# A two-layer graph network on one core: four edits to the last thirty-five microseconds

## The chip, the core and the metric

The kernel runs on one core of one Trainium2 chip. A core has TensorE (matrix products), VectorE (DVE in the profile), ScalarE (ACT), GpSimd (POOL) and SyncE (SP), each with its own queue of instructions, and DMA engines that move data between DRAM and on-chip memory. SP and ACT issue plain DMAs; POOL issues indirect ones, which gather or scatter rows by an index. The metric is the device time of one execution in microseconds (us).

## The reference

32 graphs (batches), each with 512 nodes of 512 features, share one adjacency matrix. What matters of the reference is this:

```python
def _layernorm(x): ...           # mean 0, variance 1 along the features, eps 1e-5
# layer 0
h = max(layernorm(x), 0)
x = x + (adj @ h) @ weight + bias
# layer 1: attention, 8 heads of 64 features
h = max(layernorm(x), 0)
q, k, v = h @ Wq + bq, h @ Wk + bk, h @ Wv + bv          # split into heads
scores = q k^T / 8 + (1 - adj) * -1e9
x = x + (softmax(scores) @ v) @ Wo + bo
return x                          # float32 (32, 512, 512)
```

The entries of `adj` lie between 0 and 1, and in each row of this data the largest stands well clear of the second, so the term with 1e9 leaves, in each row of scores, one node that counts. Layer 1 is then a lookup: node n takes `h[idx[n]] @ (Wv @ Wo)` plus a constant row, where `idx[n]` is the node with the largest entry in row n.

## The kernel before

The kernel first looks at `adj` and computes whether the lookup is exact for it. If so it takes `single_path`, otherwise `general_path`, a full attention. Here it takes `single_path`, and the profile is of that.

`single_path` handles one batch after another, software-pipelined. Layer 0 is two 512x512x512 products per batch. Each is done by `product`: seven products of half-size blocks with sums and differences of blocks, named p1, p5, u2, c11, c22, c12, c21. p1 opens PSUM bank u, p5 bank v and c11 a third; u2, c22 and c21 accumulate onto u, c12 onto v. After each piece, a `take` function moves the bank to its place: p1, p5, u2 and c21 with ScalarE, c11, c22 and c12 with an addition on VectorE (`take_z`, for layer 1).

Layer 1 uses the fact that only at most 352 (32 x 11) different nodes are looked up. `put_h` scatters the rows of h to DRAM so that those come first, `get_h` fetches them, `transpose_h` turns them, `layer1` computes z^T = (Wv Wo)^T h^T plus the constant into `ZT` with `product`, 176 columns at a time, `put_z` transposes z^T on VectorE into `ZR` and stores it to DRAM in four DMAs per call (one for each group of 32 partitions), for columns of blocks s0 to s1: 0 to 6 and 6 to 11. `finish` gathers the rows of z from DRAM by `place` and adds them to x. Near the end `fetch` gathers without adding, into free tiles (`late_z`: batch 29 into `sel`, batch 30 into `yT`), and `add_z` adds on VectorE and stores the batch's output.

The last batch, 31, does without that detour: `put_h` stores h unsorted, `get_all` gathers all 512 rows by `idx` into `hs[0]`, `transpose_all(r)` transposes 128 rows of it on TensorE, with a copy by ScalarE into `hs[1]`, and `layer1_rows` makes the four 128x512 row blocks of the last product, with an addition into x on VectorE and a store on SP for each.

The order of everything is written by hand, and each engine runs its instructions in the order in which they are written down. Per batch b, a list `todo` has 21 steps, seven for layer 0, seven for the next aggregation, seven for layer 1 of the batch before; `put(batch, step, f)` hangs work on a step. `run` writes down the matrix products of piece k, then the work of step k, then the `take` of piece k. In the last two rounds, b = 31 and b = 32, that gives this order:

- steps 7 to 13 of b = 31: layer 1 of batch 29. Step 13 holds `put_z(29, 6, 11)`, `get_all(31)` and two block sums; then c21 is taken by ScalarE.
- steps 14 to 20 of b = 31: layer 1 of batch 30. Step 14 (p1) holds `put_z(29, 0, 6)`, step 15 `fetch(29)`, steps 15 to 18 an addition of a constant row to x of batch 31 (`add_cvo`), step 20 (c21) `put_z(30, 6, 11)`. Step 18 belongs to c22.
- b = 32: `transpose_all(0)`, `put_z(30, 0, 6)`, `fetch(30)`, and at last `layer1_rows(31)`.

`work` is a pool with one buffer for each name: two tiles of the same name share their memory, and the second is not written before the last read of the first. `ZT` of every batch has the name "zs", and `H0S`, block sums of layer 0, "h0s". POOL's queue holds, in this order, `get_all` (four gathers), `fetch(29)` (four) and `fetch(30)` (four).

Of the kernel before, what the change touches and what calls it, by code (L numbers as in the profile page):

```python
# [8 lines left out]
F32 = mybir.dt.float32  # L9
# [8 lines left out]
P = 128  # L18
# [3 lines left out]
S = 11  # L22
# [3 lines left out]
def gnn_two_layers(ctx: ExitStack, tc: tile.TileContext, x, adj, w0, b0, wq, bq, wk, bk, wv, bv, wo, bo, out):  # L26
# [150 lines left out]
    with tc.If(single > P - 1) as cmp:  # L177
        single_path(tc, x, wv, bv, wo, bo, out, kept)
# [38 lines left out]
def single_path(ctx: ExitStack, tc: tile.TileContext, x, wv, bv, wo, bo, out, kept):  # L217
# [15 lines left out]
    nc = tc.nc  # L233
    B, N, D = x.shape
    C, DC = N // P, D // P
# [6 lines left out]
    work = ctx.enter_context(tc.tile_pool(name="work", bufs=1))  # L242
# [6 lines left out]
    PUT, H0S, H1, HS, HC, HT, HTS, Z, ZT, ZR = {}, {}, {}, {}, {}, {}, {}, {}, {}, {}  # L249
# [10 lines left out]
    def sum_a(s, t, i):  # L260
        a11, a12, a21, a22 = blk(t, 0, 0), blk(t, 1, 0), blk(t, 0, 1), blk(t, 1, 1)
        if i == 0:
            nc.vector.tensor_add(s[:, 0], a21, a22)
        elif i == 1:
            nc.vector.tensor_sub(s[:, 1], s[:, 0], a11)
        elif i == 2:
            nc.vector.tensor_sub(s[:, 2], a11, a21)
        else:
            nc.vector.tensor_sub(s[:, 3], a12, s[:, 1])
# [12 lines left out]
    def product(a, sa, bt, sb, take, half=HALF, pieces=("p1", "p5", "u2", "c11", "c22", "c12", "c21")):  # L282


        def gemm(bank, lhs, rhs, first):
            for m in range(2):
                for k in range(2):
                    nc.tensor.matmul(bank[:, m, 0:half], lhs[:, k, m * P:(m + 1) * P], rhs[:, k, :],  # L288
                                     start=(first and m == 0 and k == 0), stop=(k == 1), skip_group_check=True)

        u, v, w = None, None, None
        for piece in pieces:
            if piece == "p1":
                u = bank = ps_m.tile([P, 2, HALF], F32, name="mm")
                gemm(u, blk(a, 0, 0), blk(bt, 0, 0, half), True)
            elif piece == "p5":
                v = bank = ps_m.tile([P, 2, HALF], F32, name="mm")
                gemm(v, sa[:, 0], sb[:, 0], True)
            elif piece == "u2":
                bank = u  # L300
                gemm(u, sa[:, 1], sb[:, 1], False)
            elif piece == "c11":
                w = bank = ps_m.tile([P, 2, HALF], F32, name="mm")
                gemm(w, blk(a, 1, 0), blk(bt, 1, 0, half), True)
            elif piece == "c22":
                bank = u
                gemm(u, sa[:, 2], sb[:, 2], False)
            elif piece == "c12":
                bank = v
                gemm(v, sa[:, 3], blk(bt, 1, 1, half), False)  # L310
            else:
                bank = u
                gemm(u, blk(a, 1, 1), sb[:, 3], False)
            meanwhile = yield
            for f in meanwhile or ():
                f()
            take(piece, bank[:, :, 0:half])
# [12 lines left out]
    def take_z(t):  # L330
        def take(piece, bank):
            i, k = PLACE[piece]
            dst = blk(t, i, k, WIDE)
            if piece in ("c11", "c22", "c12"):
                nc.vector.tensor_add(dst, bank, dst)
            else:
                for m in range(2):
                    nc.scalar.activation(dst[:, m, :], bank[:, m, :], AF.Identity,  # L338
                                         bias=cvo_c[:, 2 * i + m:2 * i + m + 1])
        return take  # L340
# [75 lines left out]
    def places():  # L416
        table = dram.tile([N, 1], I32, name="table", bufs=1)
        nc.sync.dma_start(table.rearrange("(c p) o -> p (c o)", p=P), dest)
        return table

    def look_up(table):
        for c in range(C):
            nc.gpsimd.indirect_dma_start(
                out=place[:, c:c + 1], out_offset=None, in_=table,
                in_offset=bass.IndirectOffsetOnAxis(ap=idx[:, c, 0:1], axis=0))
# [67 lines left out]
    def transpose_all(r):  # L493
        pt = ps_t.tile([P, DC, P], F32, name="pt")
        for d in range(DC):
            nc.tensor.transpose(pt[:, d, :], hs[0][:, r, d * P:(d + 1) * P], ident)
        nc.scalar.copy(hs[1][:, :, r * P:(r + 1) * P], pt)
# [4 lines left out]
    def layer1_rows(b):  # L502
        for r in range(C):
            bank = ps_m.tile([P, D], F32, name="mm")
            for d in range(DC):
                if d == 2 and r + 1 < C:
                    transpose_all(r + 1)
                nc.tensor.matmul(bank, hs[1][:, d, r * P:(r + 1) * P], wvo[:, d, :], start=(d == 0), stop=(d == DC - 1))  # L508
            for bz, c in ((), ((B - 3, 0), (B - 3, 1)), ((B - 3, 2), (B - 3, 3)), [(B - 2, c) for c in range(C)])[r]:
                add_z(bz, c, nc.sync if bz == B - 3 else nc.scalar)  # L510
            x_r = X[b][:, r, :].rearrange("p (q c e) -> p q c e", q=4, c=4)
            nc.vector.tensor_add(x_r, bank.rearrange("p (c q e) -> p q c e", q=4, c=4), x_r)
            nc.sync.dma_start(out[b, r * P:(r + 1) * P, :], X[b][:, r, :])

    def transpose_h(b, r):
        if r == 0:
            HT[b] = adjT[:, :, 0:32 * S] if b == B - 2 else work.tile([P, DC, 32 * S], F32, name="hT")
        s0, s1 = 4 * r, min(4 * r + 4, S)
        nc.vector.transpose(HT[b][:, :, 32 * s0:32 * s1].rearrange("p c (s j) -> p s c j", j=32),
                            HC[b][:, s0:s1, :].rearrange("p s (c e) -> p s c e", c=4))  # L520
# [4 lines left out]
        sum_b(HTS[b], HT[b], i, WIDE)  # L525

    def layer1(b):
        ZT[b] = work.tile([P, DC, 32 * S], F32, name="zs")
        return product(wvo, wvo_t, HT[b], HTS[b], take_z(ZT[b]), WIDE)

    def put_z(b, s0, s1):
        if b not in Z:
            Z[b] = dram.tile([32 * S, D], F32, name="z")
            ZR[b] = work.tile([P, S, P], F32, name="hc" if b == B - 2 else "zr")
        nc.vector.transpose(ZR[b][:, s0:s1, :].rearrange("p s (c e) -> p s c e", c=4),  # L535
                            ZT[b][:, :, 32 * s0:32 * s1].rearrange("p c (s j) -> p s c j", j=32))
        rows = Z[b].rearrange("(s j) (q f) -> q j s f", j=32, q=4)
        for q in range(4):
            eng = nc.scalar if b == B - 2 and s0 == 0 and q > 1 else nc.sync
            eng.dma_start(rows[q][:, s0:s1, :], ZR[b][32 * q:32 * q + 32, s0:s1, :])  # L540

    def finish(b):
# [14 lines left out]
    def add_z(b, c, eng):  # L557
        nc.vector.tensor_add(X[b][:, c, :], late_z[b][:, c, :], X[b][:, c, :])
        eng.dma_start(out[b, c * P:(c + 1) * P, :], X[b][:, c, :])
# [23 lines left out]
    with tc.manual_schedule():  # L583
# [6 lines left out]
        for b in range(B + 1):  # L590
            todo = [[] for _ in range(21)]

            def put(batch, step, f, *args):
                if 0 <= batch < B:
                    todo[step].append(lambda: f(batch, *args))
# [9 lines left out]
            if b == B - 1:  # L605
                put(b - 2, 13, put_z, 6, S)
# [44 lines left out]
            put(b + 2, 17 + late, lambda b: ahead[0].offset())  # L651
            for c in range(C):
                put(b + 2, min(17 + late + c, 20), lambda b, c: ahead[0].relu(c), c)
            if b == 1:
                tables = []
                put(1, 0, lambda b: tables.append(places()))
                put(1, 11, lambda b: look_up(tables[0]))
                for step, i in ((4, 0), (4, 1), (5, 2), (5, 3)):
                    put(1, step, lambda b, i: sum_a(wvo_t, wvo, i), i)
            if b == 0:  # L660
                for step, c in ((0, 0), (0, 1), (1, 2), (2, 3)):
                    put(0, step, add_b0, c)
                for step, i in ((0, 0), (0, 1), (1, 2), (1, 3)):
                    put(0, step, lambda b, i: sum_b(adjT_s, adjT, i), i)
                todo[3] += todo[4] + todo[5] + todo[6]
                put(0, 11, lambda b: number_rows())
                for step, i in ((11, 0), (12, 1), (12, 2), (13, 3)):
                    put(0, step, lambda b, i: sum_b(w0_t, w0_s, i), i)
                for j in range(DC):
                    put(0, 16 + j, lambda b, j: bias_part(j), j)  # L670
                run(layer0_rows(0), todo[0:4])
            elif b < B:
                run(layer0(b), todo[0:7])
            else:
                transpose_all(0)
                run(None, todo[0:7])
            run(aggregate(b + 1) if b + 1 < B else layer1(b - 2) if b < B else None, todo[7:14])
            if b == 0:
# [268 lines left out]
```

## Time and profile before

| | |
|---|---|
| median of 3 runs | 1108.0 us (1107.43 to 1109.12) |
| the profiled execution | 1104.05 us |
| its span, first to last instruction | 1101.6 us |
| TensorE busy | 1079.9 us (98%) |
| VectorE busy | 907.3 us (82%) |
| ScalarE, GpSimd busy | 358.6 us (33%), 443.8 us (40%) |
| bytes moved by DMA | 186.90 MB, mean 170 GB/s |
| L288, matrix products of `product`, share of the chain that ended last | 89% |

The profile is one execution, recorded by the chip's profiler. PE is TensorE's matrix products, PEld its loading of weights; a number with L is a line of the kernel. In a row of the timeline, "[0.80 <-ACT zs L338]" says that the engine stood idle for 0.80 us and that ScalarE's line 338 ended this. A wait for several semaphores is put down to the one that came last. A DMA has two times: that of its issue on a queue (SPq, ACTq, POOL), and its landing, when all its bytes are there. The span is shorter than the execution by what lies before the first and after the last instruction, here 2.45 us.

### The profile page before, as it was taken

The page shows a single profiled execution, that of the slowest core. Times are in us where ns is not written, and L with a number is a line of the kernel's source. Part 1 is how long each engine was busy: PE and PEld are TensorE (multiplying, and loading weights), DVE is VectorE, ACT ScalarE, POOL GpSimd, SP SyncE. Part 2 cuts the span into 40 slices and gives each one's busy share as a digit, 9 for nine tenths or more (in the row PEclk, how much of TensorE's full clock was granted, in tenths as well). Part 3 has the DMA queues.
Part 4 walks back from the last instruction along what each step waited for, and adds up shares of the span by engine and source line. Part 5 has one row for each costly group of instructions (what it writes and reads, how often), then busy time and mean ns, then how long its engine had stood idle before and what let it go on. Part 6 is the DMA issues. An engine that isn't in the chain of part 4 may idle for free.

```text
span 1101.6 us, 15852 instructions
## 1 busy us (share of the span) xinstructions
PE 1079.9 (98%) x5404; PEld 953.2 (87%) x5404; DVE 907.3 (82%) x1853; ACT 358.6 (33%) x655; POOL 443.8 (40%) x491
## 2 busy tenths in 40 slices
PE   7999999999999999999999999999999999999996
PEld 3569989999989989988999998999999899999883
DVE  6869888888888888878888888888888878888863
ACT  3223323233323333322323332323332232333221
POOL 2124544333554343454333454433355434345413
PEclk9999999999999999999999999999999999999999
DMA  6362676667777667767666776666776766676537
GB/s 238 125 141 74 172 191 148 160 175 197 182 181 158 149 171 193 187 171 169 157 156 189 193 189 177 146 160 173 196 179 181 164 149 171 184 193 155 141 105 245
DMA packets 162412, 186.90 MB, mean 170 GB/s; under 512 B 14993, under 2 KB 102289, under 8 KB 162321
## 3 DMA queue, kind: packets, MB, share of 16 engines
q1 hardware_dynamic: 130672, 112.70, 37.3%
q0 software_dynamic: 27968, 66.61, 27.0%
q10 hardware_dynamic: 3680, 6.49, 1.7%
q8 instruction: 44, 0.72, 0.3%
q14 instruction: 48, 0.39, 0.2%
HBM read 96.28 MB, written 89.46 MB: 169 GB/s over the span
## 4 chain that ended last, share of the span: by engine, by line
PE 94%; DMA 1%; DVE 1%; ACT 1%; POOL 1%; issue 1%; ACTq 0%; SPq 0%; POOLq 0%; DVEq 0%
PE mm L288 89%; PE mm L139 1%; PE mm L458 1%; PE mm L372 1%; PE mm L508 1%; POOL x L544 1%; DMA x<-in_x_dram 1%; DMA yT<-z,place 1%; ACT h L212 0%; DMA z<-zr 0%; DVE x L345 0%; DVE st L194 0%; ACT zs L338 0%; POOL yT L553 0%; DVE zr L535 0%
## 5 line engine op out<-in xcount | busy, mean ns | idle before, releaser
L544 POOL DMA_INDIRECT x<-z,place x116 | 182.8, 1576 | 370.6 <-DMA z<-zr 318.7
L327 ACT COPY yT<-mm 128x512 f32<-128x512 f32 x124 | 71.8, 579 | 562.0 <-PE mm L288 527.9
L345 DVE TENSOR_TENSOR x<-mm,x 128x512 f32<-128x512 f32 x217 | 149.7, 690 | 86.2 <-PE mm L288 86.2
L212 ACT ACTIVATE h<-x,off,rstd 128x512 f32<-128x512 f32 x256 | 194.9, 808 | 36.2 <-DVE off L204 34.2
L201 POOL TENSOR_TENSOR rstd<-ve,mhalf 128x2 f32<-128x2 f32 (+1 forms) x97 | 106.0, 1093 | 222.1 <-DVE ve L200 222.1
L194 DVE BATCH_NORM_STATS2 st<-x 128x6 f32<-128x512 f32 x256 | 171.5, 670 | 9.2 <-DMA x<-in_x_dram 8.0
L288 PE MATMUL mm<-w_t,sel 128*128 128x256 f32 x744 | 171.1, 380 | 0.8 <-DVE x L345 0.8
L288 PE MATMUL mm<-adjT_s,h0s 128*128 128x256 f32 x744 | 170.8, 380 | 1.0 <-ACT yT L327 1.0
L288 PEld LDWEIGHTS mm<-w_t,sel 128*128 128x128 f32 x744 | 141.5, 191 | 20.4 <-DVE x L345 1.6
L288 PEld LDWEIGHTS mm<-adjT_s,h0s 128*128 128x128 f32 x744 | 141.6, 191 | 20.2 <-ACT yT L327 1.4
L470 POOL DMA_INDIRECT hs<-h,dest x124 | 133.7, 1078 | 30.8 <-issue 22.2
L338 ACT ACTIVATE zs<-mm,cvo_c 128x176 f32<-128x176 f32 x248 | 87.2, 403 | 98.2 <-PE mm L288 98.2
L288 PE MATMUL mm<-hTs,wvo_t 128*128 128x176 f32 x720 | 117.5, 313 | 0.6 <-ACT zs L338 0.6
L288 PE MATMUL mm<-adjT,h 128*128 128x256 f32 x496 | 117.2, 380 | 0.0
L288 PE MATMUL mm<-w_s,yT 128*128 128x256 f32 x496 | 117.2, 380 | 0.0
L288 PEld LDWEIGHTS mm<-hTs,wvo_t 128*128 128x128 f32 x720 | 109.8, 191 | 1.1 <-ACT zs L338 1.1
L288 PEld LDWEIGHTS mm<-adjT,h 128*128 128x128 f32 x496 | 94.5, 191 | 13.0 <-issue 0.5
L288 PEld LDWEIGHTS mm<-w_s,yT 128*128 128x128 f32 x496 | 93.3, 191 | 11.5 <-issue 0.5
L436 DVE TENSOR_TENSOR x<-x,b_r 128x512 f32<-128x512 f32 x128 | 86.6, 678 | 0.0
L288 PE MATMUL mm<-hT,wvo 128*128 128x176 f32 x480 | 81.4, 313 | 0.0
L288 PEld LDWEIGHTS mm<-hT,wvo 128*128 128x128 f32 x480 | 75.3, 190 | 1.5
L325 DVE TENSOR_TENSOR yT<-mm,yT 128x512 f32<-128x512 f32 x93 | 63.9, 687 | 5.8 <-PE mm L288 3.0
(146 smaller groups left out, 1278.9 us busy)
## 6 DMA issues: line engine op xcount, KB each, us to landing
out_dram<-x SPq DMA_DIRECT2D x124, 256.0 KB, 4.1
x<-in_x_dram SPq DMA_DIRECT2D x120, 256.0 KB, 5.5
hc<-hs SPq DMA_DIRECT2D x124, 176.0 KB, 3.8
z<-zr SPq DMA_DIRECT2D x120, 96.0 KB, 2.0
z<-zr SPq DMA_DIRECT2D x120, 80.0 KB, 1.9
hs<-h,dest POOLq DMA_INDIRECT x124, 5.9
x<-z,place POOLq DMA_INDIRECT x116, 5.8
x<-in_x_dram ACTq DMA_DIRECT2D x4, 256.0 KB, 5.3
```

The source lines that it names most:

```text
L139: nc.tensor.matmul(ps, hs[0][:, m, d * P:(d + 1) * P], adjT[:, m, :], start=(m == 0), stop=(m == C - 1))
L194: self.nc.vector.bn_stats(st, self.src[:, self.chunks[i], :])
L201: self.nc.gpsimd.tensor_tensor(self.rstd, ve, self.mhalf[:, 0:n], ALU.pow)
L212: self.nc.scalar.activation(dst, src, AF.Relu, bias=self.off[:, i:i + 1], scale=self.rstd[:, i:i + 1])
L288: nc.tensor.matmul(bank[:, m, 0:half], lhs[:, k, m * P:(m + 1) * P], rhs[:, k, :], start=(first and m == 0 and k == 0), stop=(k == 1), ski ...
L325: nc.vector.tensor_add(dst, bank, dst)
L327: nc.scalar.copy(dst, bank)
L338: nc.scalar.activation(dst[:, m, :], bank[:, m, :], AF.Identity, bias=cvo_c[:, 2 * i + m:2 * i + m + 1])
L345: nc.vector.tensor_add(dst, bank, dst)
L436: nc.vector.tensor_add(X[b][:, c, :], X[b][:, c, :], b0_r)
L470: stored = nc.gpsimd.indirect_dma_start(out=HS[b], out_offset=bass.IndirectOffsetOnAxis(ap=dest[:, i:i + 1], axis=0), in_=H1[b][:, i, :], ...
L544: nc.gpsimd.indirect_dma_start(out=X[b][:, c, :], out_offset=None, in_=Z[b], in_offset=bass.IndirectOffsetOnAxis(ap=place[:, c:c + 1], axi ...
```

## The change

Four edits, all of which act in the last two rounds:

- `layer1` gives z^T of batch 30 the buffer "h0s" instead of "zs", which batch 29 uses.
- `put_z` issues two of the four stores of columns 6 to 11 of batch 29 from ACT's queue instead of SP's, as it did for columns 0 to 6 of batch 30.
- `transpose_all(0)`, the first transposes of the gathered h of batch 31, is written down at step 18 of b = 31, between the products of c22 and c12 of layer 1 of batch 30, instead of after that layer.
- `layer1_rows` takes each bank and stores its rows first, and then adds z twice: batch 29 in rows 0 and 1, batch 30 in rows 2 and 3. So far the additions came ahead of the bank's: none in row 0, two of batch 29 each in rows 1 and 2, four of batch 30 in row 3.

```diff
@@ layer1_rows
                 nc.tensor.matmul(bank, hs[1][:, d, r * P:(r + 1) * P], wvo[:, d, :], start=(d == 0), stop=(d == DC - 1))
-            for bz, c in ((), ((B - 3, 0), (B - 3, 1)), ((B - 3, 2), (B - 3, 3)), [(B - 2, c) for c in range(C)])[r]:
-                add_z(bz, c, nc.sync if bz == B - 3 else nc.scalar)
             x_r = X[b][:, r, :].rearrange("p (q c e) -> p q c e", q=4, c=4)
             nc.vector.tensor_add(x_r, bank.rearrange("p (c q e) -> p q c e", q=4, c=4), x_r)
             nc.sync.dma_start(out[b, r * P:(r + 1) * P, :], X[b][:, r, :])
+            for i in range(2):
+                add_z(B - 3 + r // 2, 2 * (r % 2) + i, nc.sync if r < 2 else nc.scalar)
@@ layer1
-        ZT[b] = work.tile([P, DC, 32 * S], F32, name="zs")
+        ZT[b] = work.tile([P, DC, 32 * S], F32, name="h0s" if b == B - 2 else "zs")
@@ put_z
-            eng = nc.scalar if b == B - 2 and s0 == 0 and q > 1 else nc.sync
+            eng = nc.scalar if q > 1 and (b, s0) in ((B - 3, 6), (B - 2, 0)) else nc.sync
@@ the loop over b
+            if b == B - 1:
+                put(b, 18, lambda b: transpose_all(0))
@@ the loop over b, last round
             else:
-                transpose_all(0)
                 run(None, todo[0:7])
```

## The prediction

> **What bounds the kernel now.** I began with the page: busy times, then its chain.
>
> ```profile
> span 1101.6 us, 15852 instructions
> PE 1079.9 (98%) x5404; PEld 953.2 (87%) x5404; DVE 907.3 (82%) x1853; ACT 358.6 (33%) x655; POOL 443.8 (40%) x491
> ```
>
> TensorE bounds the kernel as a whole. But all parts of the change act after 1066 us, so the last 35 us count, and their limit may be another. I therefore took the chain of waits from 1020 us on, in order of time (start, length, what):
>
> ```profile
> 1077.78 1.98 PE mm L508 x4
> ...
> 1084.08 1.73 PE mm L508 x4
> 1085.81 0.31 issue
> 1086.12 0.94 POOL yT L553
> 1087.06 0.30 issue
> 1087.37 1.18 POOL yT L553
> 1088.54 0.30 issue
> 1088.85 5.95 DMA yT<-z,place
> 1094.79 0.02 issue
> 1094.82 0.07 DVE x L558
> 1094.88 0.54 issue
> 1095.42 0.68 DVE x L512
> ```
>
> The last thing awaited is the fourth gather of z of batch 30; two additions and a store follow it. TensorE stops at 1093.1. The step from POOL back to PE at 1086.12 is not to be believed: in the timeline each next gather of a set starts exactly 0.30 us after the one before, whatever is named as its releaser. The question is what lets the first gather go, and the timeline of 1040 to 1102 has it:
>
> ```profile
> 1069.41 1.30 ACT L338 ACTIVATE zs<-mm,cvo_c 128x176 f32<-128x176 f32 x4 [1.68 <-PE mm L288]
> 1070.17 1.46 PE L288 MATMUL mm<-adjT_s,wvo_t 128*128 128x176 f32 x8 [0.80 <-ACT zs L338]
> 1077.78 1.98 PE L508 MATMUL mm<-wvo,h 128*128 128x512 f32 x4 [0.83 <-ACT h L497]
> 1078.41 0.95 POOL L553 DMA_INDIRECT sel<-z,place  x1 [5.32 <-DMA z<-hc]
> 1084.39 1.43 POOL L553 DMA_INDIRECT yT<-z,place  x1 [1.28 <-issue]
> ```
>
> Before the gathers of 29 (into sel), POOL's queue holds a semaphore wait of 3106 ns from 1074.52 to 1077.63; before those of 30 (into yT), one of 1750 ns that ends at 1083.69. Both end when the last store of that batch's z lands: issued 1072.08, landed 5.5 us later; issued 1079.05, landed 4.6 us later. About 0.7 us after that the first gather goes. So the end hangs on stores of z, gathers of z and how the DMA engines share themselves. A table of stretches (PE, PEld, DVE, ACT, POOL busy, clock, DMA share, GB/s) shows how full they are:
>
> ```profile
> 1078.00:1084.00 6.00, 6.00 (x21) 3.04 (x21) 1.51 (x3) 0.58 (x1) 3.79 (x4) 1.00 0.86 225
> 1084.00:1095.00 11.00, 9.10 (x25) 3.93 (x23) 5.58 (x10) 1.17 (x2) 4.49 (x4) 1.00 0.97 338
> 1095.00:1099.00 4.00, 0.00 (x0) 0.00 (x0) 1.11 (x2) 0.00 (x0) 0.00 (x0) 0.74 0.62 225
> ```
>
> From 1084 to 1095 they are full. An earlier issue buys little there unless bytes move into an emptier stretch.
>
> **What the Trainium skill says.** DMA: Bandwidth & Descriptors, "Issuing engines are not separate DMA queues": all issuing queues run on the same 16 DMA engines, and a second one saves only the sequencer's issue time. The trace has that time: some 0.45 us for each store of z on SP (1067.61, 1067.98, 1068.46, 1068.95). The same page, "Queues, rings and completion order": each DMA engine takes turns between the queues that have work. The trace agrees at least that a gather's traffic slows the plain stores: stores of z land after 1.8 us at best, 5.8 us beside the gathers. Advanced Engine Details and Errata, "Sequencer and Instruction Queues", lets an instruction wait in its engine's queue for its semaphore; the trace shows that what stands behind it waits too (POOL above).
>
> **Part by part.**
>
> *Own buffer for z of 30.* Now the first four activations of layer 1 of batch 30 (two for p1, two for p5) wait until the transpose of z of 29 (1068.34 to 1069.31) has read "zs"; u2, which adds to p1's bank, then starts 0.80 us late. In "h0s", last read before 1044.25, that wait is gone: at most 0.80 us of TensorE.
>
> *Two stores of z of 29 on ACT.* They stand on ACT behind the first transpose (ends 1067.59) and ahead of c21's two activations, which now run at 1067.02. Two issues cost 0.86 us on ACT in the pair of batch 30 (1078.30 to 1079.16): ACT is free at 1068.5. The four activations of c21 and p1 then start 0.3 us apart, p1 ends at 1068.5 + 3 x 0.3 + 0.4 = 1069.8, and u2 starts at 1069.85 instead of 1070.17. So 0.3 of the 0.80 us remains. The issue of a DMA is not always so short: the fifth store on SP held its queue for 1.55 us. If ACT is held 0.86 to 3.1 us, u2 gains 0.3 or loses up to 1.9. I take 0.86, as ACT's only comparable pair.
> Behind c21 waits the second transpose of z of 29: from 1068.34 it goes to 1069.25, ending at 1070.2. SP is freed of two issues (0.9 us), but its first store after that transpose now was stuck until 1071.06. Stores from 1070.2 at 0.45 each end at 1072.0 against 1072.6 now. The last landing: nothing if the gathers of h keep the engines busy, 1.5 us if the stores find the gaps. I take 0.3 for the gathers of 29.
>
> *First transposes inside layer 1.* Four transposes (0.44 us in the chain) and one copy (0.58 us on ACT) go behind c22 of batch 30. Removed is the 0.83 us that TensorE waits for the copy. The gather that they read is issued at 1068.14 and lands 4.9 us later, at 1073.0; the transposes come at 1073.5. Half a microsecond of cover: if the gather is later, PE stands for the difference. ACT is idle 4.18 us there, so the copy is free. c12 and c21 come 0.44 - 0.3 = 0.14 us later, and with them the stores of z of 30; row 0 of the last product starts at about 1076.5 instead of 1077.78. TensorE ends 1.3 us earlier, at 1091.8. This is not the end; only the stores of rows 0 to 2 go out 1.3 us earlier, into the 0.86 stretch.
>
> *Bank ahead of z.* DVE's order so far: row 2, four additions of z of 30, row 3. Afterwards: row 2, two additions, row 3, two additions; rows 0 to 2 keep their order, and SP's and ACT's orders of stores stay. Row 3 then runs at 1091.8, as the second addition ends at 1091.75, and is done at 1092.5. The last work is the fourth addition at 1094.82 to 1095.51, its store issued at 1095.54. Now the last store is row 3's, issued 1096.13: 0.59 us less. Landing takes 3.0 us for that and 3.4 us for the other while both run; I take 3.0, and 2.5 us from landing to the span's end (1099.1 to 1101.6), which nothing changes.
>
> *The gathers of 30.* Stores of z of 30 0.14 us later: -0.1. Earlier stores of rows 0 to 2: one store is 256 KB at 338 GB/s, 0.76 us of all DMA engines; about half of it leaves the full stretch: +0.4. Row 3's store enters it instead, beside the last gathers: -0.2 (its bounds 0 and -0.76). Together +0.1, between -1 and +2.
>
> Sum: 0.6 + 0.1 = 0.7 us. Span 1101.6 to 1100.9; the profiled execution took 1104.05, so 1103.35; the median of the runs shown is 1108.0, 3.95 above that execution, and becomes 1107.3.
>
> **Rivals.** *Both z chains shorten.* If two queues let z of 29 land 1.5 us earlier, and the gathers of 29 are thus out of the way of the stores of 30, the gathers of 30 go 1.8 us earlier: with the 0.6 that is 2.4, 1105.6. For it: 1074 to 1078 has a DMA share of 0.58. Against: the two stores moved are not the late ones; c21 delays those by 0.9.
> *The engines are the wall.* The full stretch just takes row 3's store in, the last gathers land 0.6 us later, and the order on DVE gives nothing: 1108.0. For it: 0.97.
> *Slower: ACT held by its two issues.* c21, p1, u2 and everything behind them wait. Held 3.1 us (twice that fifth store) instead of 0.86, u2 starts at 1072.1, 1.9 later, the stores of 30 are 1.9 + 0.44 = 2.3 later, and the end 2.3 - 0.6 later: 1109.7. It turns slower from a hold of 1.4 us on, measurably from 3.6. Only one of 16 stores of z held its queue that long.
>
> **From numbers to chances.** A change under 0.2% (2.2 us) can't be told from none here; the runs before spread over 1.7 us. Forecast case (1106.3 to 1107.8) 0.52; engines the wall (1107.8 to 1108.8) 0.22; both chains 0.17, most of it beyond 1105.8; ACT held 0.09, half of it under 1110.2. That makes faster 0.14, same 0.81, slower 0.05. The range cuts about half of each outer case: 1105.5 to 1109.0.
>
> **What would show it.** Right: no wait of u2 for the transpose, but c21's activations near 1068.5; transposes behind c22 without a wait; the first matmul of L508 near 1076.5 without its 0.83; the last instruction on DVE an L558, not L512; the gathers of 30 still starting near 1084.4. Wrong: a wait of PE on the gather of h, DMA issues on ACT of over 1.4 us, a first gather of 30 before 1083, or a last gather that lands over 1 us from 1094.8.

## The result and the profile after

The changed kernel took 1106.57 us (median of 4 runs, 1105.23 to 1107.68) against 1108.44 us for the kernel before (4 runs as well; the 1108.0 us further up is the median of the first three). The ratio is 0.9983, with a 95% interval from 0.9966 to 1.0001. In a second series with more runs (below) it was 0.9992, from 0.9983 to 1.0000. A gain of one or two microseconds is likely, and neither interval is clear of none.

The profiled execution took 1105.83 us. The page's first lines:

```profile
span 1103.6 us, 15851 instructions
PE 1081.1 (98%) x5404; PEld 952.3 (86%) x5404; DVE 908.0 (82%) x1853; ACT 358.9 (33%) x655; POOL 443.9 (40%) x491
```

This span is 2.0 us longer than that of before, although the median is shorter. Both traces run the same instructions until 1057 us, but from about 100 us on this one is late: ScalarE stands idle there for 3.63 us where the trace of before has 0.67 us, and for the rest of the way it stays between 3 and 4.7 us late. Spans of single executions therefore can't be compared. I measure the tail instead, from the first product of layer 1 of batch 29 (1057.61 us before, 1061.52 us after) to the end of the span: 44.0 us before, 42.1 us after. All times called "T +" below count from that product. To set a row of this trace beside one of before, take 3.91 us off.

The chain that ended last (start, length, what):

```profile
1073.28 0.50 issue
1073.78 3.85 PE mm L288 x24
1077.63 0.44 PE pt L496 x4
1078.06 2.39 PE mm L288 x16
1080.45 1.72 PE mm L508 x4
...
1091.03 0.95 POOL yT L553
1091.97 0.30 issue
1092.28 6.31 DMA yT<-z,place
1098.58 0.02 issue
1098.61 0.69 DVE x L558
```

The end is still the fourth gather of z of 30. Behind it now stands one addition, L558, not two. The transposes (L496) sit inside layer 1, and L508 follows with no wait for the copy. The timeline has the rest:

```profile
1071.53 0.85 ACTq L540 DMA_DIRECT2D z<-zr  x2
1072.42 0.71 ACT L338 ACTIVATE zs<-mm,cvo_c 128x176 f32<-128x176 f32 x2 [4.03 <-DVE adjT_s L278]
1073.78 1.46 PE L288 MATMUL mm<-adjT_s,wvo_t 128*128 128x176 f32 x8 [0.50 <-issue]
1080.29 1.88 PE L508 MATMUL mm<-wvo,h 128*128 128x512 f32 x4
1080.84 0.94 POOL L553 DMA_INDIRECT sel<-z,place  x1 [3.62 <-PE mm L288]
1088.11 0.94 POOL L553 DMA_INDIRECT yT<-z,place  x1 [2.58 <-DMA out_dram<-x]
```

ACT's two stores hold c21 (second row), u2 waits 0.50 us instead of 0.80, and L508 starts at T + 18.8 instead of T + 20.2. The first gather of 29 goes at T + 19.3 (before: 20.8), the first of 30 at T + 26.6 (before: 26.8). The stretches that answer to those of before (PE, PEld, DVE, ACT, POOL busy, clock, DMA share, GB/s):

```profile
1081.91:1087.91 6.00, 6.00 (x21) 3.11 (x20) 2.28 (x4) 1.17 (x2) 2.83 (x3) 1.00 0.99 266
1087.91:1098.91 11.00, 7.59 (x21) 3.24 (x19) 5.81 (x9) 0.59 (x1) 4.19 (x4) 1.00 0.99 349
1098.91:1102.91 4.00, 0.00 (x0) 0.00 (x0) 0.39 (x1) 0.00 (x0) 0.00 (x0) 0.56 0.39 143
```

The DMA share of the first stretch has risen from 0.86 to 0.99, that of the last has fallen from 0.62 to 0.39: bytes did move forward.

But the parts don't add up to 2.0 us. The last store leaves its queue at T + 37.8 instead of T + 38.5, which is the 0.7 us of the forecast. The other 1.3 us come after it: from the issue of the last store to the end of the span it is 5.5 us before, and 4.2 us after. The forecast had this stretch unchanged. Here are the issue of the last store, the last branches of the two queues, which lead to the closing instructions, and the closing instructions themselves (count, shortest/median/longest in ns, first and last start), first of before:

```profile
L513 SPq DMA_DIRECT2D out_dram<-x x1: 332/332/332, 1096.1 to 1096.1; - x1
...
L177 ACTq COMPARE_BRANCH  x1: 38/38/38, 1096.3 to 1096.3; - x1
L177 SPq COMPARE_BRANCH  x1: 43/43/43, 1096.5 to 1096.5; - x1
...
L942 SPq EVENT_SEMAPHORE  x14: 17/28/28, 1100.0 to 1101.6; - x14
```

and of after:

```profile
L559 ACTq DMA_DIRECT2D out_dram<-x x1: 338/338/338, 1099.3 to 1099.3; - x1
...
L177 SPq COMPARE_BRANCH  x1: 43/43/43, 1096.6 to 1096.6; - x1
...
L177 ACTq COMPARE_BRANCH  x1: 38/38/38, 1099.7 to 1099.7; - x1
...
L943 SPq EVENT_SEMAPHORE  x14: 17/28/28, 1099.6 to 1103.5; - x14
...
L943 ACTq DRAIN  x2: 8/44/80, 1102.7 to 1103.0; - x2
```

Between the end of the branch and the first closing instruction some 3 us pass on each of the two queues: 3.4 us on SP before, 2.9 us on SP and on ACT after. Then SP waits for the semaphores of the DMAs one after the other, which takes it to 1100.7 before. In the kernel before SP also issues the last store, so its 3.4 us and its checks come behind one another, behind that store. After the change SP is through with its branch at 1099.6, before the last landing, and only ACT's branch follows the last store. This became the theory to test, called "end"; its first rival, "gathers", puts the gain down to the earlier stores and gathers of z.

### The profile page after: what moved, and what is told of

Read it like the earlier page. It is cut to its first block, busy times and chain, and to the rows that moved or that the text cites. A ratio compares the mean times of both kernels' runs of the same rounds, so it can differ in the third digit from the quotient of the medians.

```text
span 1103.6 us, 15851 instructions
## 1 busy us (share of the span) xinstructions
PE 1081.1 (98%) x5404; PEld 952.3 (86%) x5404; DVE 908.0 (82%) x1853; ACT 358.9 (33%) x655; POOL 443.9 (40%) x491
## 4 chain that ended last, share of the span: by engine, by line
PE 94%; DVE 2%; DMA 1%; ACT 1%; POOL 1%; issue 1%; another core or an unknown queue 0%; ACTq 0%; SPq 0%; POOLq 0%; DVEq 0%
PE mm L288 88%; PE mm L139 1%; PE mm L458 1%; PE mm L372 1%; PE mm L508 1%; DMA yT<-z,place 1%; POOL x L544 1%; DMA x<-in_x_dram 1%; ACT h L212 0%; DMA z<-zr 0%; DVE x L345 0%; DVE st L194 0%; ACT yT L327 0%; ACT zs L338 0%
## 5 line engine op out<-in xcount | busy, mean ns | idle before, releaser
L288 PEld LDWEIGHTS mm<-w_t,sel 128*128 128x128 f32 x744 | 141.1, 190 | 20.8 <-DVE x L345 1.6
L338 ACT ACTIVATE zs<-mm,cvo_c 128x176 f32<-128x176 f32 x240 | 84.6, 404 | 98.4 <-PE mm L288 90.7
```

## Experiments

Unless a run says otherwise, ratios are to the kernel before in one series of runs, in which that kernel took 1103.8 to 1104.0 us (medians).

**The order alone.** The kernel before with the new `layer1_rows`:

```diff
-            for bz, c in ((), ((B - 3, 0), (B - 3, 1)), ((B - 3, 2), (B - 3, 3)), [(B - 2, c) for c in range(C)])[r]:
-                add_z(bz, c, nc.sync if bz == B - 3 else nc.scalar)
...
             nc.sync.dma_start(out[b, r * P:(r + 1) * P, :], X[b][:, r, :])
+            for i in range(2):
+                add_z(B - 3 + r // 2, 2 * (r % 2) + i, nc.sync if r < 2 else nc.scalar)
```

> The kernel before with the new order in layer1_rows alone; z of 30 stays in zs, all stores of z of 29 stay on SP, the first transposes stay behind layer 1. Measured from the first product of layer 1 of batch 29 to the end of the span (before: 44.0 us, after: 42.0 us). Theory 'end' (the span ends a fixed time after the queue that issues a store last: 5.5 us after SP's, 4.2 us after ACT's): row 3's store leaves SP by 36.5 us, ACT's last store goes at 37.9 us as before, so the end comes at 42.1 to 42.2: nearly the whole gain. Rival 'gathers' (earlier gathers made the gain, the order is worth the 0.6 us of the forecast): 43.4.

Measured: ratio 0.9992 (0.9983 to 1.0000), 0.7 us in the median; end at T + 42.8, between the two numbers. ACT's last store went at T + 37.9 as said, but the end followed 4.9 us later, not 4.2. The order alone gives about as much as the whole change does in this series (0.9992 as well, below).

**All but the order.** The changed kernel with the old lines of `layer1_rows`, the reverse of the diff above.

> The changed kernel with the old order in layer1_rows, the other three edits kept. From the first product of layer 1 of batch 29 to the end. Theory 'end': the last store is row 3's on SP, some 0.1 us earlier than in the kernel before, so 43.8 to 44.0. Rival 'gathers': 42.6.

Measured: ratio 1.0000 (0.9991 to 1.0008). In time this is what "end" says. The trace says something else: its last store left SP at T + 37.2, 1.3 us earlier than in the kernel before, and it ended at T + 42.4. I return to how little one trace is worth.

**The very last store on SP.** One edit on top of the changed kernel:

```diff
-                add_z(B - 3 + r // 2, 2 * (r % 2) + i, nc.sync if r < 2 else nc.scalar)
+                add_z(B - 3 + r // 2, 2 * (r % 2) + i, nc.sync if r < 2 or (r == 3 and i == 1) else nc.scalar)
```

> The changed kernel, but the very last store (rows 384 to 511 of batch 30) goes out on SP instead of ACT; nothing else. Theory 'end': the end follows SP's last store by 5.5 us instead of ACT's by 4.2: 43.2 to 43.4. Rival 'landing' (the end follows the last landing by a fixed time, whatever the queue): 42.0 to 42.2.

Measured: the end at T + 43.3, in one execution. The store left at T + 37.7, 0.1 us earlier than ACT's in the changed kernel, and the end came 5.6 us later, as "end" has it. Its branches and closing instructions:

```profile
L177 SPq COMPARE_BRANCH  x1: 43/43/43, 1095.5 to 1095.5; - x1
...
L943 SPq EVENT_SEMAPHORE  x14: 17/28/28, 1099.1 to 1100.7; - x14
```

SP's 3.6 us and its checks are behind the last store again. Over all traces of this study: where SP issues the last store (before twice, all but the order, this one, two queues alone below) the end follows by 5.1 to 5.7 us, mean 5.4; where ACT does (the other nine), by 4.2 to 5.2 us, mean 4.6. So the end does follow ACT's store sooner, but by 0.8 us on average, not by the 1.3 us of the first two traces. What this alone is worth in median time was not measured: the kernel of this section ran once (1102.93 us).

**All stores of z of 29 on SP.** The changed kernel with `put_z` as it was:

```diff
-            eng = nc.scalar if q > 1 and (b, s0) in ((B - 3, 6), (B - 2, 0)) else nc.sync
+            eng = nc.scalar if b == B - 2 and s0 == 0 and q > 1 else nc.sync
```

> The changed kernel with all stores of z of 29 on SP again. If ACT's two issues hold c21 (as the trace of after reads), c21 runs 1.5 us earlier relative to the first product of layer 1 of 29 (9.4 us after it instead of 10.9), and u2 of batch 30 starts without a wait, 0.5 us earlier (11.8 instead of 12.3). If the second queue is what lands z of 29 1.5 us earlier, the first gather of 29 falls back from 19.3 to about 20.8 us after that product; if it came from something else, it stays by 19.3. End: theory 'end' 42.0 to 42.3, as the last gathers hardly move; rival 'gathers' 43 or more if the gathers of 29 fall back.

Measured: c21 at T + 9.4, as expected, and u2 straight behind p5, without a wait, at T + 11.6. The first gather of 29 went at T + 20.3, which speaks for the second queue landing z sooner; but the first gather of 30 went at T + 26.2, earlier than in the changed kernel. End at T + 43.0 in one execution.

**Before and after once more.** To see what a trace is worth, both kernels unchanged.

> The changed kernel itself, once more, for the size of its gain beside the single edits and for how far one execution's last 44 us repeat. Theory 'end' with its order alone at -0.7 us in the median: the other three edits add little, so -0.7 to -1.2 us against the kernel before. Rival 'gathers': the two traces of before and after show a gain of 2.0 us behind the first product of layer 1 of 29, and if the earlier first gather of 29 (19.3 against 20.8 us) is the change's own doing, it repeats, and the gain is 1.7 to 2.2 us.

> The kernel before itself, for one more trace. If the time at which the stores of z of 29 land is a matter of chance in each execution, the first gather of 29 goes 0.5 us or more away from the 20.8 us (after the first product of layer 1 of 29) of the first trace: with the order alone it went at 18.6, though nothing ahead of it differs from before. If it is the program's own, it goes at 20.6 to 21.0. Either way the last store leaves on SP, and the end follows 5.1 to 5.6 us later (theory 'end').

Measured: the changed kernel has ratio 0.9992 (0.9983 to 1.0000), 0.9 us in the median, inside the range of "end" and below that of "gathers". It ends at T + 42.0, nearly as in its first trace (42.1), 4.5 us behind its last store. The kernel before ends at T + 43.6, 5.1 us behind it. The two traces of each kernel agree on the tail to 0.5 us; the kernels are 1.7 us apart there on average, about twice what the runs of this series show. The first gather of 29 in the kernel before went at T + 20.4, 0.4 us off its first trace: undecided by the bounds set. The pairs below decide it.

**ACT's two stores behind c21.** They stay on ACT, but one step later:

```diff
-        for q in range(4):
+        for q in range(2 if (b, s0) == (B - 3, 6) else 4):
...
+    def put_rest(b):
+        rows = Z[b].rearrange("(s j) (q f) -> q j s f", j=32, q=4)
+        for q in range(2, 4):
+            nc.scalar.dma_start(rows[q][:, 6:S, :], ZR[b][32 * q:32 * q + 32, 6:S, :])
...
                 put(b - 2, 13, put_z, 6, S)
+                put(b - 2, 14, put_rest)
```

> The changed kernel, but ACT issues its two stores of z of 29 behind c21's activations instead of ahead of them. c21 goes back to 9.4 us after the first product of layer 1 of 29, the second transpose of z of 29 ends 0.9 us earlier, u2 of batch 30 starts at 11.8 without its 0.5 us wait, TensorE ends 0.5 us earlier. Theory 'end' (the last 6 us hang on the last gather of 30, and that on full DMA engines): within 0.4 us of the changed kernel. Rival 'hold' (ACT's hold costs the change its gain on TensorE): 0.5 to 1.0 us faster than the changed kernel.

> The kernel with ACT's two stores of z of 29 behind c21's activations, once more. Its median was 2.2 us under the kernel before, 1.3 us under the changed kernel, but its trace ended as late after the first product of layer 1 of 29 (42.2 us) as that of the changed kernel (42.0). If the median was right (rival 'hold'), the ratio to before is 0.997 to 0.9985 again. If the trace was right (theory 'end'), it is 0.999 to 0.9995, as of the changed kernel. First gather of 29 and of 30: seesaw, see the next run.

Measured: 0.9981 (0.9970 to 0.9993), and again 0.9981 (0.9973 to 0.9990). The two medians lie 1.3 and 0.9 us under that of the changed kernel, as the rival "hold" had it, though the intervals overlap with that kernel's 0.9983 to 1.0000; the first trace, which ended no earlier (T + 42.2), misled. The two executions of this one kernel also show chance at work. POOL's first gathers, first run:

```profile
1078.40 0.94 POOL L558 DMA_INDIRECT sel<-z,place  x1 [5.11 <-DMA z<-hc]
...
1084.15 0.94 POOL L558 DMA_INDIRECT yT<-z,place  x1 [1.06 <-DMA out_dram<-x]
```

second run, whose first product of layer 1 of 29 stands only 0.08 us later:

```profile
1076.07 0.94 POOL L558 DMA_INDIRECT sel<-z,place  x1 [2.70 <-DMA z<-zr]
...
1086.48 0.94 POOL L558 DMA_INDIRECT yT<-z,place  x1 [5.73 <-DMA out_dram<-x]
```

Of the same program, the first gather of 29 goes 2.3 us earlier and the first of 30 2.3 us later. In the 14 traces, four have the first gather of 29 at T + 20.3 or later, and their first of 30 lies at T + 26.2 to 26.8; ten have it before T + 19.6, and their first of 30 lies at T + 26.6 to 28.6. It fits that early gathers of 29 run beside the stores of z of 30 and hold those up ("seesaw" in the next expectation); this was not tested by itself. What tips it in an execution was not found.

**One queue for z of 29, timed.** The same kernel as two runs above.

> The changed kernel with all stores of z of 29 on SP, now timed. Theory 'seesaw': whatever lets the gathers of 29 start earlier sends them into the stores of z of 30, and the gathers of 30 then start later, so two queues for z of 29 give nothing at the end: this is within 0.4 us of the changed kernel (0.999 to 0.9996 of before), and a first gather of 29 after 20 us goes with a first gather of 30 before 26.8. Rival: two queues help, and without them the kernel falls back to 0.9996 to 1.0002 of before.

Measured: 0.9977 (0.9969 to 0.9984), 2.2 us in the median: the fastest kernel here. The rival falls (two queues don't help), and so does the size that "seesaw" gave: it is not within 0.4 us of the changed kernel but 1.3 us faster, and with 18.9 and 26.6 this execution has both gathers early. ScalarE and TensorE, where the changed kernel holds them:

```profile
1067.83 0.71 ACT L338 ACTIVATE zs<-mm,cvo_c 128x176 f32<-128x176 f32 x2 [2.54 <-PE mm L288]
...
1068.83 2.55 PE L288 MATMUL mm<-adjT_s,wvo_t 128*128 128x176 f32 x16
...
1076.42 1.88 PE L508 MATMUL mm<-wvo,h 128*128 128x512 f32 x4
```

p5 and u2 are one run of 16 products, with no gap. Together with the kernel that issues the same two stores on ACT behind c21 (0.9981 both times), this tells two causes apart, as far as the overlapping intervals allow: a second queue costs little or nothing, c21 held behind it costs about 1 us. The traces don't show this difference: those of the one-queue kernel end at T + 41.9 and 43.0, those of the changed kernel at 42.1 and 42.0.

**Two queues for z of 29 alone**, on the kernel before:

```diff
-            eng = nc.scalar if b == B - 2 and s0 == 0 and q > 1 else nc.sync
+            eng = nc.scalar if q > 1 and (b, s0) in ((B - 3, 6), (B - 2, 0)) else nc.sync
```

> The kernel before with two stores of z of 29 on ACT and nothing else. Forecast's step (ACT's two issues hold c21 by 1.5 us, the second transpose by 0.9): with the shared buffer zs, p1's activations of batch 30 wait for that transpose, so they run at 12.6 us after the first product of layer 1 of 29 instead of 11.7, u2 at 13.4 instead of 12.6, and TensorE ends 0.8 us later, at 36.3. Then row 3 on SP may become the last by its bank: 37.0 at the earliest, which is still ahead of the last gather's 37.2. End 43.6 to 44.6, ratio to before 0.9998 to 1.0006. Rival 'two queues help': first gather of 29 at 19 to 19.3 and end below 43.2.

Measured: 1.0015 (1.0008 to 1.0021), 1.5 us slower; end at T + 45.1.

```profile
1068.06 0.85 ACTq L540 DMA_DIRECT2D z<-zr  x2
1068.96 0.70 ACT L338 ACTIVATE zs<-mm,cvo_c 128x176 f32<-128x176 f32 x2 [4.03 <-DVE adjT_s L278]
1070.77 1.31 ACT L338 ACTIVATE zs<-mm,cvo_c 128x176 f32<-128x176 f32 x4 [1.11 <-DVE zr L535]
...
1071.53 1.46 PE L288 MATMUL mm<-adjT_s,wvo_t 128*128 128x176 f32 x8 [1.72 <-ACT zs L338]
```

The hold is what was expected: p1 at T + 12.7, u2 at T + 13.5, TensorE's end at T + 36.4. What was not expected is that it reaches the end in full and more. The last addition, which waits for the last gather of 30, started at T + 38.1, against 37.2 and 37.1 in the traces of before. The gathers of 29 start early (T + 19.3) without any use.

**First transposes back behind layer 1.** The changed kernel without that edit:

```diff
-            if b == B - 1:
-                put(b, 18, lambda b: transpose_all(0))
...
             else:
+                transpose_all(0)
                 run(None, todo[0:7])
```

> The changed kernel with the first transposes behind layer 1 of batch 30 again. TensorE then waits 0.83 us for the copy, starts L508 at about 19.9 us after the first product of layer 1 of 29 instead of 18.8, and ends at 35.1 instead of 34.0. Forecast's step (TensorE's end is not the end): the last store still leaves ACT at 37.5 to 38.0, end 42.0 to 42.6, ratio to before as of the changed kernel. Rival (earlier stores of rows 0 to 2 relieve the full stretch): last gather 0.4 us later, end 42.5 to 43.

Measured: 0.9996 (0.9988 to 1.0004). L508 started at T + 19.9 and TensorE ended at T + 35.2, as said. The end did not come at T + 42.0 to 42.6 but at 43.5: the last addition started at T + 37.6, 0.5 and 0.8 us later than in the traces of the changed kernel, and the last store sat 1.1 us in its issue on ACT. The median is 0.5 us worse than the changed kernel's, and the intervals overlap. Whether TensorE's 1.2 us count for a little at the end stays open.

**Two output stores later.** On the kernel with ACT's stores behind c21; `add_z` issues no store where it is given None:

```diff
-                add_z(B - 3 + r // 2, 2 * (r % 2) + i, nc.sync if r < 2 else nc.scalar)
+                add_z(B - 3 + r // 2, 2 * (r % 2) + i, None if r == 1 else nc.sync if r < 2 else nc.scalar)
+        for c in range(2, C):
+            nc.sync.dma_start(out[B - 3, c * P:(c + 1) * P, :], X[B - 3][:, c, :])
```

> The kernel of the run before with two of the four stores of the output of batch 29 issued on SP behind row 3's, out of the way of the gathers of 30. If the full DMA engines set when the last gather lands, 512 KB less beside it bring it 0.5 to 1.0 us earlier, and the kernel is 0.3 to 0.8 us faster than without this, as SP, which now issues until about 36 us, ends 5.4 us later, ahead of ACT. Rival: gathers and stores don't wait for each other (the gathers are bound by their own queue): no difference, or slower where the two late stores land last.

Measured: 0.9992 (0.9985 to 0.9998), against 0.9981 without it; the median is 1.3 and 0.8 us above the two of that kernel. The expectation failed: 512 KB taken away from beside the gathers did not speed the kernel up but slowed it down. In its one trace the first gather of 30 started at T + 28.3, late by the seesaw, so the trace can't tell whether the gathers themselves went faster. The end came 5.2 us behind ACT's last store, the longest such time of the nine traces in which ACT issues last. It fits that the two late stores, issued 2.2 and 1.7 us before that store, run beside it; this was not tested.

## Why the prediction was right, and where it was not

The time was 1107.3 forecast, 1106.57 measured; "not to be told from no change" was the likeliest verdict and is what the intervals say. By its own steps:

- *u2 and the hold by ACT.* Forecast: c21 at 1068.5, u2 at 1069.85. Less 3.91 us, the trace after has 1068.51 and 1069.87. Right. The 0.80 us of idle time understated what u2 can gain: with neither wait it starts at T + 11.6, 1.0 us before its start in the kernel before, so the hold takes 0.7 us from it (T + 12.3), not 0.5.
- *First transposes.* Forecast: L508 from about 1076.5, TensorE's end at 1091.8. Measured, less 3.91 us: 1076.4 and 1091.6. Right, with no wait for the gather of h. The half microsecond of cover is as thin as the forecast said: in the first trace with ACT's stores behind c21 TensorE waited 0.4 us for that gather.
- *Bank ahead of z.* Forecast 0.59 us. The trace has the last store 0.7 us earlier, and the order alone measured 0.7 us. That is right in size, with an interval from nothing to 1.9 us. One term was wrong: "2.5 us from landing to the span's end, which nothing changes". Issuing the last store on ACT instead of SP brings the end 0.8 us closer to that store, on average over 14 traces. So a part of what this edit brings may come from there, and much of the 2.0 us between the first two traces does.
- *Gathers.* Forecast: the first gather of 30 about where it was, "+0.1, between -1 and +2". T + 26.6 and 27.4 in the two traces of after, 26.8 and 26.2 in those of before: two executions of one kernel differ by more than the forecast's +0.1.
- *Two stores of z of 29 on ACT.* Here a step failed. By the forecast's own working the hold takes back 0.5 of the 0.80 us that the buffer wins for u2, and against it stand 0.3 us for the gathers of 29; neither has a term in the sum, which has only the net of all edits for the stores of z of 30, 0.14 us later. That net is what the trace shows (the first of them leaves SP at T + 19.3, before at 19.1), but it hides what this edit alone costs. Without it the kernel is 0.9977 instead of 0.9992; alone it makes the kernel 1.5 us slower. The edit costs about 1.3 us. The hold passes from c21 and u2 to the last products of layer 1 of 30, and so to the stores of z of 30, which leave ACT at T + 20.0 without the edit, T + 20.7 with it (as in the kernel before), and T + 21.6 with it alone. Up to here the traces show it. That it reaches the end through the gathers of 30, which wait for those stores, is argued: the last addition starts at T + 37.0 and 37.9 in the traces without the edit, and at 37.1 and 36.8 in those of the changed kernel. That a delay of 0.8 or 0.9 us shows as 1.3 or 1.5 us is within the intervals of one for one; whether more is behind it was not settled.

So the total was right in part by luck. The forecast put everything but the order at 0.1 us, and together it is not much more: 0.9 us for the whole change less 0.7 us for the order, and 0.3 us for the change without the order. But two larger parts cancel in it. If the parts add, the buffer and the transposes, which no run had alone, bring about 1.5 us (2.2 us without ACT's stores, less 0.7 us for the order), and ACT's stores take most of that back.

The forecast's slower rival named the right mechanism, ACT held by its issues. It looked for the loss only where the hold exceeds 0.86 us, and the measured hold of 0.85 us already costs. The rival "both chains shorten" falls: the kernel with one queue for z of 29 is faster than that with two. "The engines are the wall" is neither shown nor excluded.

## What to carry to other kernels

A DMA issued from a compute engine's queue costs that queue its issue time and its wait, in front of whatever compute stands behind (here c21 ran 1.5 us later, 0.6 us of it the wait of the stores); ask where that compute's result goes before calling the time free. Leaving that one edit out gives 0.9977 (0.9969 to 0.9984), faster than before and clear of noise, where the whole change gives 0.9992. When a tail hangs on DMA landings, one trace of each kernel does not order two kernels that differ by a microsecond: runs do.

## What the runs showed of the hardware

- From the end of its last branch (40 ns long itself) to its first closing instruction SP took 2.9 to 3.7 us in 13 traces and 5.1 us in one, ACT 2.9 to 3.6 us in all 14. The span ended 4.2 to 5.2 us after a last store on ACT, 5.1 to 5.7 us after one on SP.
- In two executions of one program, the first gather of 29, which waits for the stores of z, started at T + 18.2 and T + 20.6, with issues on SP and POOL within 0.7 us of each other up to there.
